# Edge rows added in pairs on VectorE before the one-hot products, in a graph-attention layer on one core

## The chip, the cores and the metric

The kernel runs on one core of one Trainium2 chip. The metric is the device time of one launch in microseconds; the time before is the median of three runs. Engines are named as the profile names them: PE is TensorE, DVE is VectorE, ACT is ScalarE, POOL is GpSimd, SP is SyncE.

## The reference

12,500 nodes with 128 features and 412,500 directed edges, sorted by their target node. A layer norm and a ReLU precede a graph attention with four heads of 32; the result is added to x.

```python
h = relu(layernorm(x)) @ W_node.T             # per head: 32 columns
att = sum(concat(h[src], h[dst], edge_attr @ W_edge.T) * a)   # one number per edge and head
att = where(att > 0, att, 0.2 * att)
m = maximum(segment_max(att, dst), 0)
ex = exp(att - m[dst])
denom = segment_sum(ex, dst) + (num_edges - deg) * exp(-m)
out = x + segment_sum(ex / denom[dst] * h[src], dst)
```

The sources are random, so h[src] is a gather of 412,500 rows.

## The kernel before

**Lead-in.** All 98 blocks of 128 nodes are loaded, measured with bn_stats on DVE, normalized on ACT and POOL, transposed on PE, passed through a ReLU on DVE, multiplied with the weights and written to a table in DRAM. A row of the table (ROW = 144 numbers) has, per head, 32 features, two ones and two parts of the attention. The lead-in is a software pipeline over units of three blocks, its order written out by hand: a unit is normalized and transposed three steps (`lag`) ahead of its product. Only when the table is complete can the first row be gathered.

**Batches.** The edges come in 461 chunks of 896. Seven chunks make a batch; there are 66 batches, the last with six chunks. Of a batch, POOL gathers the rows of the sources: one indirect DMA for each group of 128 edges, 49 in a batch (`gather`, L631), 3223 in all. Each reads its 128 row numbers from the tile `ends` in SBUF. Four buffers (`hs`) hold gathered batches, and POOL runs through batch after batch with one short memset (`gate`) between them, which waits for the products of the batch that had the buffer before.

When the rows of a batch have landed, DVE adds the attention parts (`logits`, L729), finds each node's highest attention with two scans (L739, L741), ACT takes the exponentials (L744), DVE makes a one-hot of each edge's target modulo 32 (`mark`, L699), weights the rows (`scatter`, L814), and PE multiplies the one-hot with the rows: seven groups, two products each, 14 in a batch (L819). The sums go to DRAM and come back turned (`pass_on`, `turn_sums`). `choose` picks the target's part of the next batch's attention by predicated copies (L606). DVE runs all of that in program order.

**Merge.** Two batches at a time, `merge` carries sums across chunks with a scan, writes each chunk's last value into two places (`put`, L919), and adds them with one DVE instruction per chunk at a column read from a register (L926). `finish` divides and adds x when a group of nodes is complete: L1002 multiplies with a factor in PSUM, L1005 adds two tiles in SBUF, L866 shifts the sums.

**Where tiles lie.** `exr`, `up` of the batches, `more`, `pa` and `z` are in PSUM; `hs`, `ends`, `acc`, `xg`, `a`, `hot` and `pick` are in SBUF. In the row `hs<-hs,exr` of L814 one input is therefore in SBUF and one in PSUM, in `xg<-xg,a` of L1005 both are in SBUF.

**The end.** The last batch is done in two parts (four groups of each chunk, then three), so that the first part's attention and sums run while the second part is still gathered.

Should a chunk break an assumption on the lists (sortedness, how far targets spread), a flag is raised and a slow loop over windows does the whole work again at the end.

Of the kernel before, what the change touches and what calls it, by code (L numbers as in the profile page):

```python
# [65 lines left out]
COUNTED = 24  # L66
FIRST = 2
# [58 lines left out]
def kernel(  # L126
# [3 lines left out]
    ends: bass.AP,  # L130
    dstc: bass.AP,
# [37 lines left out]
    lastm = const.tile([P, NC2, 2], U8, name="lastm")  # L169
# [28 lines left out]
    for b in range(NBT):  # L198
        if b == NBT - 1 or base_of(b + 1) > base_of(b):
            c = chunk_of(b + 1) - 1  # L200
            nc.gpsimd.memset(highest[:, c:c + 1], float(base_of(b) + WQ - 2))
# [35 lines left out]
    with (  # L237
# [50 lines left out]
        def extent(g):  # L288
# [7 lines left out]
            nc.sync.dma_start(pens[g * P:g * P + n, :], pen[:n, :])  # L296
            nc.vector.tensor_reduce(ext[:n, g, 0:1], dch[:n, :], AX.X, OP.min)
            nc.vector.tensor_reduce(ext[:n, g, 1:2], rise[:n, :], AX.X, OP.min)
            nc.vector.tensor_reduce(ext[:n, g, 2:3], dch[:n, :], AX.X, OP.max)
# [4 lines left out]
        sizes = [XS, XS, 2 * XS] + [XB] * ((NB - 4 * XS) // XB)  # L304
        sizes += [XS, NB - sum(sizes) - XS]
# [51 lines left out]
        def normalize(u):  # L357
            s = u.s
            u.hn = p2.tile([P, XS, D], F32, name="hn", bufs=4)
# [39 lines left out]
        def keep_near():  # L399

            pn = pp1.tile([P, H * P], F32, name="pn")[:NB, :].rearrange("p (h i) -> p h i", h=H)
# [18 lines left out]
        ahead, lag = 7, 3  # L420
# [3 lines left out]
        measure(units[1])  # L424
# [23 lines left out]
        def chunk_ranges():  # L448
# [4 lines left out]
            pb = [pp1.tile([P, H * P], F32, name="pn")[:, :NC2], pp1.tile([P, NC2], F32, name="pb")]  # L453
# [30 lines left out]
            yield  # L484
            nc.vector.tensor_tensor(qn, qn, later, op=OP.add)
# [6 lines left out]
            nc.vector.tensor_tensor(lastm[:, :, 1], last, later, op=OP.mult)  # L492
            nc.vector.tensor_tensor(lastm[:, :, 0], last, lastm[:, :, 1], op=OP.subtract)
# [3 lines left out]
        done = 2  # L497
        full = None
        for k in range(-lag, whole + 1):
# [3 lines left out]
            u = units[k + lag] if k + lag < whole else None  # L503
            if 0 <= k < whole:
                project(units[k])
            if u:
                normalize(u)
                turn(u)
                if u is u.s.units[-1]:
                    load_next()  # L510
            if full:
                write(full)
            full = keep_rows(units[k]) if 0 <= k < whole else None
            for _ in range(2):
                if done < min(k + ahead + 1, whole):
                    measure(units[done])
                    done += 1
            if u:
                keep_turned(u)
            for s in measured:  # L520
                root(s)
            measured.clear()
            if k == whole - 4:
                early += [index(b) for b in range(2, AHEAD)]
        keep_near()
        load_extents()
# [17 lines left out]
    here_ps = more_ps[:, LEVELS * T * CB:LEVELS * T * CB + MC * 2].rearrange("p (c j) -> p c j", j=2)  # L544
# [138 lines left out]
    def mark(s):  # L683

        if s.b < NBT - 1:
            s.hot = work.tile([P, T, CB, W], F32, name="hot", bufs=2)
        else:
            s.hot = work.tile([P, SB, CE], F32, name="eft").rearrange("p j e -> p (j e)")[
                :, :T * CB * W].rearrange("p (t q r) -> p t q r", q=CB, r=W)
        dk = work.tile([P, CB * T], I32, name="dk")  # L690
        dst = s.ends[:, :, 1, :]
        nc.vector.tensor_scalar(dk.rearrange("p (q t) -> p q t", t=T), dst, W - 1, None, op0=OP.bitwise_and)

        far = work.tile([P, CB * T], F32, name="far")
        nc.vector.tensor_scalar(far, away, float(W), float(W), op0=OP.is_ge, op1=OP.mult)
        key = work.tile([P, T * CB], F32, name="key")
        nc.vector.tensor_tensor(key.rearrange("p (t q) -> p q t", q=CB), far.rearrange("p (q t) -> p q t", t=T),
                                dk.rearrange("p (q t) -> p q t", t=T), op=OP.add)
        nc.vector.tensor_tensor(s.hot.rearrange("p t q r -> p (t q) r"), rows_ps[:, None, :].to_broadcast([P, T * CB, W]),  # L699
                                key[:, :, None].to_broadcast([P, T * CB, W]), op=OP.is_equal)  # L700

    def weigh(s):
# [7 lines left out]
        weigh_part(s, 0, EARLY if s.b == NBT - 1 else T)  # L710

    def open_weights(s):

        s.zst = work.tile([P, T, R], F32, name="zst")
        s.att = work.tile([P, BUF], F32, name="a")[:R, :CE]
        s.up = ps.tile([P, BANKS * 512], F32, name="up")[:R, :CE]
        s.m = work.tile([P, BUF], F32, name="m")[:R, :CE]
        s.both = work.tile([P, 2, T, R], F32, name="both")

    def weigh_part(s, t0, t1):  # L720

        zst, att, up, m, both = s.zst, s.att, s.up, s.m, s.both
        own = s.hs.rearrange("p (t q) (h k) -> p t q h k", t=T, h=H)[:, t0:t1, :s.chunks, :, AW - 1]
        e0, e1 = t0 * P, t1 * P

        def grouped(what, g):
            return what.rearrange("r (t g i) -> r g t i", g=NQT, i=R)[:, g, t0:t1, :]

        nc.vector.tensor_tensor(logits[:, t0:t1, :s.chunks * H].rearrange("p t (q h) -> p t q h", h=H),  # L729
                                own, s.pick[:, t0:t1, :s.chunks, :H], op=OP.add)  # L730
        nc.vector.transpose(zst[:, t0:t1, :].rearrange("p t i -> p (t i)"),
                            logits[:, t0:t1, :].rearrange("p t i -> p (t i)"))
# [9 lines left out]
        on_half(s, nc.vector.tensor_tensor(att[:, e0:e1], z, mp, op=OP.subtract))  # L742
        for g in range(NQT):
            nc.scalar.activation(both[g * R:(g + 1) * R, 0, t0:t1, :], grouped(att, g), AF.Exp)  # L744
        for g in range(NQT):
            nc.vector.scalar_tensor_tensor(both[g * R:(g + 1) * R, 1, t0:t1, :], grouped(s.pen[:, 1:], g), -1.0 / BIG,  # L746
                                           grouped(up, g), op0=OP.mult, op1=OP.mult)
        if t1 - t0 == T:
            nc.vector.transpose(both_ps.rearrange("p w t r -> p (w t r)"), both.rearrange("p w t r -> p (w t r)"))
        else:  # L750
            for w in range(2):
                nc.vector.transpose(both_ps[:, w, t0:t1, :].rearrange("p t r -> p (t r)"),
                                    both[:, w, t0:t1, :].rearrange("p t r -> p (t r)"))
        nc.vector.tensor_copy(own, both_ps[:, 1, t0:t1, :s.chunks * H].rearrange("p t (q h) -> p t q h", h=H))
# [17 lines left out]
    def first_part(s):  # L772
# [6 lines left out]
        weigh(s)  # L779
        s.first = sum_part(s, *spans[0])  # L780
# [27 lines left out]
    def scatter(s):  # L808
# [3 lines left out]
        for t0, t1 in ((0, FIRST), (FIRST, T)):  # L812
# [3 lines left out]
            for t in range(t0, t1):  # L816
                for g in range(2):
# [598 lines left out]
```

## Time and profile before

| | us |
|---|---|
| three runs | 4144.61, 4147.24, 4148.44 |
| median | 4147.24 |
| the profiled execution | 4155.16 |
| its span, first to last instruction | 4153.4 |
| DVE busy | 2397.3 (58%) |
| POOL busy | 3093.9 (74%) |
| PE busy | 1362.1 (33%) |
| ACT busy | 461.3 (11%) |

The profile's durations come from the one profiled execution, whose time is 7.9 us over the median of the runs and 1.8 us over its own span. "Idle before" in a row is the time in which the engine did nothing ahead of these instructions, with what ended it.

### The profile page before, as it was taken

To read this page: it belongs to the slowest core of one execution; us is meant where nothing else is said; L and a number is where in the kernel's file an instruction comes from. 1 tells how busy PE (TensorE), PEld (TensorE's weight loads), DVE (VectorE), ACT (ScalarE), POOL (GpSimd) and SP (SyncE) were. 2 spreads that over 40 slices of the span, in tenths; PEclk is the share of its full clock that TensorE was granted. 3 is DMA by queue.
4 is the path that set the end of the run, shared out by engine and by line. 5 is a ranking of instruction groups with operands and counts; after the bars stand their busy time and mean duration, and the time that the engine had idled before them with its cause. 6 is when DMAs were issued, how large, how long until landed. Compare 5 with 4: busy or idle time off the path is not lost.

```text
span 4153.4 us, 18432 instructions
## 1 busy us (share of the span) xinstructions
PE 1362.1 (33%) x3375; PEld 539.4 (13%) x3375; DVE 2397.3 (58%) x3550; ACT 461.3 (11%) x654; POOL 3093.9 (74%) x3393
## 2 busy tenths in 40 slices
PE   5332333233233233233323323323323322332331
PEld 4111111011011011111101101101101110110111
DVE  7456465456556457646555655654655654665576
ACT  4011011011101101101101110110110110111011
POOL 4777777777777777777777777777777777777775
PEclk8665666666666666566666666656656666666665
DMA  6443443443343444334444434444434434434442
GB/s 182 137 113 97 108 121 94 112 118 101 103 121 99 112 112 118 100 108 114 95 112 119 105 103 114 103 110 113 114 100 114 117 91 112 119 99 113 119 106 55
DMA packets 417256, 457.11 MB, mean 110 GB/s; under 512 B 240614, under 2 KB 324794, under 8 KB 417132
## 3 DMA queue, kind: packets, MB, share of 16 engines
q0 software_dynamic: 103136, 237.83, 24.2%
q1 hardware_dynamic: 199232, 165.73, 14.0%
q10 hardware_dynamic: 114764, 52.30, 4.7%
q14 instruction: 96, 0.79, 0.1%
q8 instruction: 28, 0.46, 0.0%
HBM read 406.51 MB, written 49.05 MB: 110 GB/s over the span
## 4 chain that ended last, share of the span: by engine, by line
POOL 73%; issue 24%; DVE 2%; PE 0%; DMA 0%; ACT 0%; POOLq 0%; ACTq 0%; SPq 0%; DVEq 0%
POOL hs L631 73%; DVE stats L331 0%; DVE hT L377 0%; POOL gate L627 0%; DMA turned<-wide 0%; DVE acc L926 0%; PE pt L372 0%; PE ph L382 0%; PE pa L803 0%; ACTq L841 0%; POOLq L631 0%; DMA hs<-table,ends 0%; DVE dif L340 0%; DVE tot L337 0%; DVE dif L341 0%
## 5 line engine op out<-in xcount | busy, mean ns | idle before, releaser
L631 POOL DMA_INDIRECT hs<-table,ends x3223 | 3059.0, 949 | 990.6 <-issue 975.6
L819 PE MATMUL pa<-hs,hot 128*128 128x504 f32 x1820 | 929.5, 676 | 2673.1 <-DVE hs L814 2673.1
L729 DVE TENSOR_TENSOR logits<-hs,pick 128x196 f32<-128x196 f32 x65 | 32.4, 499 | 1497.8 <-DVEq L648 1497.8
L819 PEld LDWEIGHTS pa<-hs,hot 128*128 128x128 f32 x1820 | 396.4, 222 | 3198.4 <-issue 3166.3
L814 DVE TENSOR_TENSOR hs<-hs,exr 128x1848 f32<-128x1848 f32 (+1 forms) x130 | 451.6, 3516 | 0.0
L744 ACT ACTIVATE both<-a 32x224 f32<-32x224 f32 (+2 forms) x268 | 103.2, 385 | 2593.7 <-DVE a L742 2583.4
L679 PE MATMUL z<-eft,wa 128*32 128x512 f32 (+1 forms) x792 | 319.6, 547 | 6.3 <-DMA eft<-in_ef 6.3
L606 DVE COPY_PREDICATED pick<-more,pick 128x1568 f32<-128x1568 int32 (+3 forms) x260 | 253.6, 975 | 8.9
L606 DVE COPY_PREDICATED pick<-more,lw 128x3136 f32<-128x3136 int32 x65 | 241.3, 3712 | 9.5 <-ACT pick L590 3.8
L590 ACT COPY pick<-lw 128x3136 f32<-128x3136 f32 x65 | 182.4, 2806 | 11.5 <-ACTq L648 9.9
L926 DVE TENSOR_TENSOR acc<-acc,up 128x70 f32 x461 | 105.2, 228 | 71.0 <-issue 52.0
L739 DVE TENSOR_TENSOR_SCAN up<-pen_sb,z 32x896 f32<-32x896 f32 (+1 forms) x67 | 133.6, 1994 | 2.3
L741 DVE TENSOR_TENSOR_SCAN m<-pen_sb,up 32x896 f32<-32x896 f32 (+1 forms) x67 | 132.6, 1979 | 2.3
L699 DVE TENSOR_TENSOR hot<-exr,key 128x1568 f32<-128x1568 f32 x65 | 116.5, 1792 | 2.3
L734 DVE TENSOR_TENSOR up<-z,zst 32x224 f32<-32x224 f32 (+2 forms) x268 | 104.3, 389 | 13.8
L679 PEld LDWEIGHTS z<-eft,wa 128*32 128x32 f32 x792 | 79.5, 110 | 242.1 <-issue 235.0
L746 DVE SCALAR_TENSOR_TENSOR both<-pen_sb,up 32x224 f32<-32x224 f32 (+2 forms) x268 | 100.2, 374 | 4.3
L856 ACT COPY r<-turned 128x245 f32<-128x245 f32 x65 | 41.5, 639 | 339.0 <-ACTq L648 295.9
L738 DVE TENSOR_TENSOR z<-up,a 32x896 f32<-32x896 f32 (+1 forms) x67 | 72.3, 1080 | 2.3
L742 DVE TENSOR_TENSOR a<-z,m 32x896 f32<-32x896 f32 (+1 forms) x67 | 71.7, 1070 | 2.3
L737 DVE TENSOR_SCALAR a<-up 32x896 f32<-32x896 f32 (+1 forms) x67 | 71.3, 1064 | 2.3
L676 PE MATMUL z<-eft,wa 128*64 128x512 f32 (+1 forms) x132 | 64.6, 571 | 21.3 <-DMA eft<-in_ef 21.3
(181 smaller groups left out, 900.3 us busy)
## 6 DMA issues: line engine op xcount, KB each, us to landing
eft<-in_ef SPq DMA_DIRECT2D x33, 1792.0 KB, 8.2
hs<-table,ends POOLq DMA_INDIRECT x3223
eft<-in_ef SPq DMA_DIRECT2D x33, 1344.0 KB
wide<-stage ACTq DMA_DIRECT2D x65, 504.0 KB, 2.9
lw<-near SPq DMA_DIRECT2D x461, 64.0 KB
pen_sb<-pens SPq DMA_DIRECT2D x66, 98.1 KB
table<-rows ACTq DMA_DIRECT2D x9, 648.0 KB, 3.6
xg<-in_x SPq DMA_DIRECT2D x52, 112.0 KB, 6.1
```

Of the source, the lines that this page charges most:

```text
L590: nc.scalar.copy(s.pick[:, :, :s.chunks, :], lw[:, None, :s.chunks, :n].to_broadcast([P, T, s.chunks, n]))
L606: nc.vector.copy_predicated(s.pick[:, :, :s.chunks, :n], bit[:, :, :, None].to_broadcast([P, T, s.chunks, n]), more)
L631: load = nc.gpsimd.indirect_dma_start(out=s.hs[:, t * CB + q, :], out_offset=None, in_=table[:, :], in_offset=bass.IndirectOffsetOnAxis(ap ...
L679: s.made = own_half(s, nc.tensor.matmul(s.z[:, part], wa3[:, j + s.b % 2 * (SB + 1), :], s.eft[:, j, part], start=False, stop=(j == NEXT - ...
L699: nc.vector.tensor_tensor(s.hot.rearrange("p t q r -> p (t q) r"), rows_ps[:, None, :].to_broadcast([P, T * CB, W]), key[:, :, None].to_br ...
L734: on_half(s, nc.vector.tensor_tensor(grouped(up, g), grouped(s.z, g), zst[g * R:(g + 1) * R, t0:t1, :], op=OP.add))
L739: on_half(s, nc.vector.tensor_tensor_scan(up[:, e0:e1], s.pen[:, e0:e1], z, 0.0, op0=OP.add, op1=OP.max))
L741: nc.vector.tensor_tensor_scan(mp[:, ::-1], s.pen[:, e1:e0:-1], up[:, e0:e1][:, ::-1], 0.0, op0=OP.add, op1=OP.max)
L744: nc.scalar.activation(both[g * R:(g + 1) * R, 0, t0:t1, :], grouped(att, g), AF.Exp)
L814: nc.vector.tensor_tensor(rows, rows, ex_ps[:, t0:t1, :CB * H, None].to_broadcast([P, t1 - t0, CB * H, HB]), op=OP.mult)
L819: scattered[s.b] = nc.tensor.matmul(wide_ps[:, g, :], s.hot[:, t, g * NEXT:g * NEXT + SB, :].rearrange("p q r -> p (q r)"), flat[:, at:at ...
L926: nc.vector.tensor_tensor(sums, sums, put[:, i0 + i, :, :], op=OP.add)
```

## The change

1. **Lists.** For all but the last batch, the host lays the edges of a chunk out so that a partition's seven edges are neighbours in the sorted order (edge 7p + t instead of 128t + p). The number of gathers is unchanged. The edges' attention on the other side of the transpose is reordered with strided views (`grouped`).
2. **Products.** As neighbours mostly share a target, and a partition's seven edges change target at most once (checked by a new flag in `extent`), DVE adds the rows of edges 1, 3, 5 onto those of 0, 2, 4; the products of edges 0, 2, 4 and 6 follow. Where the two of a pair differ, the odd rows, kept by a 0/1 factor (`split`), are added up, and a fifth product moves them from the first target to the last: its one-hot is the difference of those of edge 6 and edge 0. Five rounds of two products replace seven. `mark` makes four one-hots and a difference instead of seven one-hots.
3. **Weights.** The four DVE additions of attention per batch become four ACT copies and one DVE addition; the four exponentials on ACT become four ACT copies and one exponential after the transpose back; the four products with the penalty become one.
4. **Merge.** A table of zeros and ones (`rel`, `one`) over eight columns replaces the writes per chunk: per batch one product of 128x1960, one reduction to 128x280, one addition to `acc`.
5. **Order.** `mark` moves ahead of the scans, `choose` of the next batch ahead of the transpose back.
6. **Lead-in.** An older form: two steps ahead instead of three, fewer buffers, other sizes of the first and last groups, other order within a step.

```diff
-        sizes = [XS, XS, 2 * XS] + [XB] * ((NB - 4 * XS) // XB)
-        sizes += [XS, NB - sum(sizes) - XS]
+        sizes = [XS, 2 * XS] + [XB] * ((NB - 3 * XS) // XB)
+        sizes += [2 * XS, NB - sum(sizes) - 2 * XS]
...
-            u.hn = p2.tile([P, XS, D], F32, name="hn", bufs=4)
+            u.hn = p2.tile([P, XS, D], F32, name="hn", bufs=3)
...
-            pt = pps.tile([P, XS, P], F32, name="pt", bufs=3)
+            pt = pps.tile([P, XS, P], F32, name="pt")
...
-            u.hT = p2.tile([P, XS, P], F32, name="hT", bufs=5)
+            u.hT = p2.tile([P, XS, P], F32, name="hT", bufs=3)
...
-        ahead, lag = 7, 3
+        ahead = 8
...
     def mark(s):
...
+            nc.vector.tensor_tensor(s.hot[:, ROUNDS - 1, :, :], s.hot[:, ROUNDS - 2, :, :], s.hot[:, 0, :, :], op=OP.subtract)
+            s.split = work.tile([P, T // 2, CB], F32, name="split")
+            nc.vector.tensor_tensor(s.split, dk[:, 1::2, :], dk[:, 0:T - 1:2, :], op=OP.not_equal)
...
         for g in range(NQT):
-            on_half(s, nc.vector.tensor_tensor(grouped(up, g), grouped(s.z, g),
-                                               zst[g * R:(g + 1) * R, t0:t1, :], op=OP.add))
+            nc.scalar.copy(grouped(s, s.pair[:, 0:1, :], g, t0, t1)[:, 0], s.zst[g * R:(g + 1) * R, t0:t1, :])
...
+        on_half(s, nc.vector.tensor_tensor(up[:, e0:e1], z, att[:, e0:e1], op=OP.add))
...
+        nc.vector.scalar_tensor_tensor(mp, s.pen[:, e0 + 1:e1 + 1], -1.0 / BIG, up[:, e0:e1], op0=OP.mult, op1=OP.mult)
         for g in range(NQT):
-            nc.scalar.activation(both[g * R:(g + 1) * R, 0, t0:t1, :], grouped(att, g), AF.Exp)
-        for g in range(NQT):
-            nc.vector.scalar_tensor_tensor(both[g * R:(g + 1) * R, 1, t0:t1, :], grouped(s.pen[:, 1:], g), -1.0 / BIG,
-                                           grouped(up, g), op0=OP.mult, op1=OP.mult)
+            nc.scalar.copy(both[g * R:(g + 1) * R, :, t0:t1, :], grouped(s, s.pair, g, t0, t1))
...
+        nc.scalar.activation(ex_ps[:, t0:t1, :], ex_ps[:, t0:t1, :], AF.Exp)
...
     def scatter(s):
...
-            for t in range(t0, t1):
-                for g in range(2):
...
+        tiles = flat.rearrange("p (t c) -> p t c", t=T)
+        add_to(s, T - 1, ROUNDS - 2, True)
+        nc.vector.tensor_tensor(tiles[:, 0:T - 1:2, :], tiles[:, 0:T - 1:2, :], tiles[:, 1::2, :], op=OP.add)
+        for k in range(ROUNDS - 2):
+            add_to(s, 2 * k, k)
+        odd = s.hs.rearrange("p (t q) c -> p t q c", t=T)[:, 1::2, :, :]
+        nc.vector.tensor_tensor(odd, odd, s.split[:, :, :, None].to_broadcast([P, T // 2, CB, ROW]), op=OP.mult)
+        for k in range(1, T // 2):
+            nc.vector.tensor_tensor(tiles[:, 1, :], tiles[:, 1, :], tiles[:, 2 * k + 1, :], op=OP.add)
+        add_to(s, 1, ROUNDS - 1)
+
+    def add_to(s, t, k, start=False):
...
+        for g in range(2):
+            at = (t * CB + g * NEXT) * ROW + g * HALFROW
+            scattered[s.b] = nc.tensor.matmul(
+                wide_ps[:, g, :], s.hot[:, k, g * NEXT:g * NEXT + SB, :].rearrange("p q r -> p (q r)"),
+                flat[:, at:at + SPAN], start=start, stop=(k == ROUNDS - 1))
...
-            for i, v in enumerate(got):
-                sums = acc[:, ds(v, 2), :]
-                nc.vector.tensor_tensor(sums, sums, put[:, i0 + i, :, :], op=OP.add)
...
+        for i, v in enumerate(got):
+            spread_out = work.tile([P, 2, BUF], F32, name="a").rearrange("p w c -> p (w c)")[
+                :, :JW * AW * each].rearrange("p (j d c) -> p j d c", j=JW, d=AW)
+            ends_of = val[:, :, step + i * CB * step:1 + (i * CB + each) * step:step]
+            nc.vector.tensor_tensor(spread_out, ends_of[:, None, :, :].to_broadcast([P, JW, AW, each]),
+                                    one[:, i, :, None, :each].to_broadcast([P, JW, AW, each]), op=OP.mult)
+            nc.vector.tensor_reduce(put, spread_out, AX.X, OP.add)
+            sums = acc[:, ds(v, JW), :]
+            nc.vector.tensor_tensor(sums, sums, put, op=OP.add)
```

More of the change, by code (lines that the diff above doesn't have):

```diff
@@ L502 @@
             rooted.clear()
-            u = units[k + lag] if k + lag < whole else None
             if 0 <= k < whole:
                 project(units[k])
[L506 to L519, printed above, removed]
+            if k + 2 < len(units):
+                normalize(units[k + 2])
             for s in measured:
@@ L695, in mark @@
[L695 to L698, printed above, removed]
+            s.hot = work.tile([P, ROUNDS, CB, W], F32, name="hot", bufs=2)
+            dk = work.tile([P, T, CB], I32, name="dk")
+            nc.vector.tensor_scalar(dk.rearrange("p t q -> p q t"), s.ends[:, :, 1, :], W - 1, None, op0=OP.bitwise_and)
@@ L1033, in close @@
             return
[L1034 removed]
+        merge(first, chunk_of(first), chunks_of(first, last), *merged.pop(first))
         for b0, n, behind in parts():
```

197 lines of the change are left out of this document (122 added, 75 removed).

## The prediction

> **What bounds the kernel now.** I read the page first: the span, the chain of work that ended last, and the costliest groups.
>
> ```profile
> span 4153.4 us, 18432 instructions
> ...
> POOL 73%; issue 24%; DVE 2%; PE 0%; DMA 0%; ACT 0%; POOLq 0%; ACTq 0%; SPq 0%; DVEq 0%
> ...
> L631 POOL DMA_INDIRECT hs<-table,ends x3223 | 3059.0, 949 | 990.6 <-issue 975.6
> L729 DVE TENSOR_TENSOR logits<-hs,pick 128x196 f32<-128x196 f32 x65 | 32.4, 499 | 1497.8 <-DVEq L648 1497.8
> ```
>
> POOL's gathers and the issue gaps between them are 97% of the chain. DVE, the engine on which most of the change lies, stands idle 1497.8 us ahead of its first instruction of a batch, 23 us in each of 65, because the rows have not landed. The line of the gathers says how rigid this is:
>
> ```profile
> L631 POOL DMA_INDIRECT hs<-table,ends x3223: 943/947/1841, 77.4 to 4118.1; - x190
> ```
>
> 3222 steps from 77.4 to 4118.1 are 1.254 us each; the median gather is 0.947 and the gap 975.6/3222 = 0.303, together 1.250. So the time is lead-in 77.4, then 3223 gathers back to back, then a tail of 4153.4 - 4119.1 = 34 us. Four products fewer on PE, or less DVE work, buy nothing in the middle. The question is whether anything in the change touches the gathers, and a few of them did take up to 1841 ns. The timeline shows when.
>
> ```profile
> 1231.99 1.09 DVE L1002 TENSOR_TENSOR a<-acc,exr 128x896 f32<-128x896 f32 x1
> 1232.59 0.95 POOL L631 DMA_INDIRECT hs<-table,ends  x1 [0.30 <-issue]
> 1233.11 1.09 DVE L1005 TENSOR_TENSOR xg<-xg,a 128x896 f32<-128x896 f32 x1
> 1233.84 1.18 POOL L631 DMA_INDIRECT hs<-table,ends  x1 [0.30 <-issue]
> ```
>
> The gather that starts inside L1002 (one input in SBUF, `exr` in PSUM) takes 0.95; the one that starts inside L1005 (both inputs in SBUF) takes 1.18. It ends at 1235.02, 0.82 after L1005's end at 1234.20. A second place, with a copy right behind:
>
> ```profile
> 863.82 1.09 DVE L1005 TENSOR_TENSOR xg<-xg,a 128x896 f32<-128x896 f32 x1
> 863.92 1.82 POOL L631 DMA_INDIRECT hs<-table,ends  x1 [0.31 <-issue]
> 864.83 0.56 DVE L866 COPY acc<-acc 128x770 f32<-128x770 f32 x1
> ```
>
> ```profile
> 619.53 0.55 DVE L866 COPY acc<-acc 128x770 f32<-128x770 f32 x1
> 619.73 1.16 POOL L631 DMA_INDIRECT hs<-table,ends  x1 [0.30 <-issue]
> ```
>
> The gather of 863.92 ends at 865.74, again 0.83 after L1005's end (864.91), although L866 had begun by then, and L866 does hold a gather that starts inside it (1.16 at 619.73, end 0.81 after the copy's). So: a gather that starts inside such an instruction is held until that instruction ends, gets through before the next one, and ends 0.82 later, as if it had started 0.12 before the end. L1005 itself loses nothing. The long weighting products, with `exr` in PSUM, hold nothing:
>
> ```profile
> 4086.25 6.94 DVE L814 TENSOR_TENSOR hs<-hs,exr 128x1848 f32<-128x1848 f32 x2
> 4086.83 0.95 POOL L631 DMA_INDIRECT hs<-table,ends  x1 [0.30 <-issue]
> 4088.08 0.95 POOL L631 DMA_INDIRECT hs<-table,ends  x1 [0.30 <-issue]
> ```
>
> Thus POOL loses, for a DVE instruction of length L with two SBUF inputs, L - 0.12 - s, where s is the time from its start to the next gather's start; nothing if that is negative. For a random phase s is between 0 and 1.25, 0.63 in the mean.
>
> **The change part by part.** Its new instructions with two SBUF inputs need lengths.
>
> ```profile
> L926 DVE TENSOR_TENSOR acc<-acc,up 128x70 f32 x461 | 105.2, 228 | 71.0 <-issue 52.0 <-DVE acc L926 4.7
> ...
> L919 DVE TENSOR_TENSOR up<-up,more 128x476 f32<-128x476 f32 x62 | 59.9, 967 | 2.1
> ...
> L1005 DVE TENSOR_TENSOR xg<-xg,a 128x896 f32<-128x896 f32 x13 | 14.2, 1095 | 0.5
> ...
> L1005 DVE TENSOR_TENSOR xg<-xg,a 128x512 f32<-128x512 f32 x1 | 0.7, 691 | 0.0
> ```
>
> L1005's two sizes give (1095 - 691)/384 = 1.05 ns an element and 0.15 us besides: 3.33 us for 3024 elements, 2.21 for 1960, 1.21 for 1008, 0.39 for 224.
>
> *The pairs (the term that decides).* Each of 65 batches gets four in a row on `hs`, all from SBUF: the pair addition (3024), the product with `split` (3024), and two additions of 1008. The first costs POOL 3.33 - 0.12 - 0.63 = 2.58 (1.96 to 3.21 by the phase, which is likely the same in every batch, since DVE starts each at the landing of its last gather). The held gather ends 0.83 after it, the next starts 0.30 later, at 1.13; the second instruction begins some 0.03 after the first (L1002 to L1005), so s is 1.10 and the loss 3.33 - 0.12 - 1.10 = 2.11. At the third, s is 1.10 again against 1.21 - 0.12 = 1.09: free by a hair, as is the fourth (0 to 0.1 each if that is off). Sum 4.69 a batch, 65 x 4.69 = **305 us**, all on POOL's chain, since nothing can catch up a gather.
>
> [...]
>
> *The merge.* The product of 1960 per batch reads `val` and `one`, both SBUF: 2.21 - 0.12 - 0.63 = 1.46 (0.84 to 2.09). The views step through short runs, and L919, with a strided view, took 967/476 = 2.0 ns an element; at that rate it is 4.1 us and 3.3 lost. I take the lower, as the innermost run of seven is contiguous. 64 of the 66 fall while POOL still gathers: 64 x 1.46 = **93 us** (54 to 211). The reduction reads one input, `acc` is added to PSUM: no loss; the additions of L926, with one PSUM input too, go at no gain on the chain.
>
> *Small ones.* The one-hot difference (0.39 us) holds a gather only when one starts in its first 0.27: 0.27²/2.5 = 0.03 a batch. With the third and fourth additions above and three passes of 468 in the lead-in: **3 us**.
>
> *DVE itself.* How much room it has:
>
> ```profile
> 620.00:1110.00 490.00, 163.79 (x336) 61.55 (x336) 276.36 (x374) 50.31 (x65) 371.69 (x400) 0.65 0.42 109
> ```
>
> Eight batches of 61.3 us hold 34.6 us of DVE each. Added: 9.1 for the four, and per batch 2.2 + 2.2 + 0.4 in the merge in place of 7 x 0.228 + 0.97; the shorter one-hots and single additions return one or two. Some 46 of a period that becomes 67: hidden. If this cover were gone, DVE would set the period, and it is 20 us away. `choose` and `mark` ahead of the transpose delay the rest of the batch's DVE work but no gather: the buffer POOL needs next belongs to a batch three back. ACT's eight copies lie beside that. The products removed on PE wait for DVE anyway: nothing.
>
> *Lead-in.*
>
> ```profile
> 20.00:30.00 10.00, 7.28 (x53) 6.35 (x54) 8.25 (x42) 6.87 (x17) 3.93 (x9) 1.00 0.58 163
> ```
>
> DVE is busy 8.25 of 10 here and keeps the same instructions, so a better order could give at most 0.18 x 60 = 10 us; an order with two steps instead of three between transpose and product, and fewer buffers, can only wait more: I take +4, with -5 and +20 as ends. The new passes of `extent` run while POOL gathers.
>
> *Tail.* After the last batch's first rows land, DVE and ACT take turns:
>
> ```profile
> 4102.10 0.33 DVE L729 TENSOR_TENSOR logits<-hs 128x96 f32<-128x96 f32 x1 [8.63 <-DVEq L648]
> ...
> 4108.75 1.15 DVE L746 SCALAR_TENSOR_TENSOR both<-pen_sb,up 32x128 f32<-32x128 f32 x4
> 4108.75 0.31 ACT L744 ACTIVATE both<-a 32x128 f32<-32x128 f32 x1 [5.30 <-DVE a L742]
> ...
> 4115.64 0.64 ACT L856 COPY r<-turned 128x245 f32<-128x245 f32 x1 [5.62 <-ACTq L648]
> ...
> 4119.92 1.20 DVE L919 TENSOR_TENSOR up<-up,more 128x238 f32<-128x238 f32 x2
> 4121.15 1.81 DVE L926 TENSOR_TENSOR acc<-acc,up 128x70 f32 x7
> ```
>
> The 9.1 us of additions of the batch before fit the 8.63 of idle time, the more so as the rows land later. Then ACT's four copies (some 0.31 each) come ahead of one addition (about 0.7 for 512), in place of four additions: +1; the penalty product now comes ahead of ACT's copies and a transpose ahead of the exponential, and the transfers of `turn_sums` are behind that on ACT: +3 until L856. The merge: 2.2 + 2.2 + 0.4 for 1.2 + 1.8: +1.7. The second part pays about 2 and its merge 1.5. Sum **+9** (2 to 14).
>
> **Sum.** Against the profiled execution: 4155.2 + 305 + 93 + 3 + 4 + 9 = 4569. That execution is 7.9 over the median of the runs, so the median should come to 4147.2 + 414 = **4561**. About 0.2%, 8 us, is what a measurement of this kernel can tell from no change.
>
> **The rivals.**
>
> *Each of the four costs its whole length.* POOL is not let in between neighbouring instructions, or a waiting DVE instruction takes the next turn. Then the four cost 9.1 - 0.12 - 0.63 = 8.3 a batch: 4147 + 540 + 93 + 16 = **4796**. Against it: the gather of 863.92 got through before L866, and L1005 took the same 1.09 wherever gathers lay. For it: no row shows two such instructions of equal kind in a row.
> [...] Chance 0.10.
>
> *No loss: the other side.* The place is the four instructions on `hs` and the product in the merge, the price of each zero, if a gather's reading of `ends` can be served beside them; it decides as soon as gathers started inside them still take 0.95. What L1005 showed would then be something of L1005 alone, such as the stores issued after it. Then the time is 4147 + 13 - 7 = **4153** with little of lead-in and tail, not slower.
> [...] Chance 0.04.
>
> *It does not do what it says.* If the lists broke the new flags, the slow loop would do everything again, thousands of us. In the reference's lists, which I counted, no partition changes target twice and no batch spans more than eight windows. Chance 0.01.
>
> **How the numbers follow.** The forecast has 0.85. Its own ends: 65 x (1.96 + 2.0) + 64 x 0.84 - 5 + 2 gives 4455; 65 x (3.21 + 2.3) + 211 + 20 + 14 gives 4750. The corner needs the strided rate and the worst phase together, so I cut it: 4455 to 4700 holds about 0.8 of all cases, with the two main rivals outside. Faster 0.01, within 0.2% 0.03 (the second rival, which could come out a little on either side), slower 0.96.
>
> **What would show it.** In the profile after, the gathers keep a median of 0.947 but their mean rises from 0.949 to about 1.07 (0.949 + 401/3223), with two long ones a batch, ending 0.82 after the pair addition and the `split` product, and one in each merge; the step between gathers is 1.38 instead of 1.25; DVE's idle time ahead of the attention parts stays near 20 us a batch; POOL and issue still make nearly the whole chain. I am wrong on the mechanism if gathers inside those instructions take 0.95, on its size if none passes between them or if the merge's product takes over 3 us.

## The result, and the profile after

The changed kernel takes 4515.01 us (median of four runs, 4512.01 to 4517.71) against 4146.65 for the kernel before beside it: a ratio of 1.0888 (1.0869 to 1.0907), 368 us slower. The forecast was 4561 in a range of 4455 to 4700.

The page after, its lines of the span, of the gathers and of DVE's wait ahead of a batch, then the line of the gathers (shortest, median and longest of one in ns, first and last start):

```profile
span 4514.5 us, 16833 instructions
...
L657 POOL DMA_INDIRECT hs<-table,ends x3223 | 3408.2, 1057 | 984.8 <-issue 984.8
L757 DVE TENSOR_TENSOR logits<-hs,pick 128x196 f32<-128x196 f32 x65 | 32.4, 499 | 1249.0 <-DVEq L674 1249.0
```

```profile
L657 POOL DMA_INDIRECT hs<-table,ends x3223: 940/944/4081, 75.0 to 4464.4; - x190
```

The median gather is 0.944 us, as before (0.947); the mean has gone from 0.949 to 1.057. POOL still waits for nothing but its own issue gaps. DVE still idles 1249/65 = 19 us a batch. So the loss is inside single gathers, and the timeline of a batch shows in which:

```profile
1035.61 3.37 DVE L861 TENSOR_TENSOR hs<-hs 128x3024 f32<-128x3024 f32 x1
1035.65 0.95 POOL L657 DMA_INDIRECT hs<-table,ends  x1 [0.31 <-issue]
...
1036.90 2.91 POOL L657 DMA_INDIRECT hs<-table,ends  x1 [0.30 <-issue]
...
1039.02 3.31 DVE L865 TENSOR_TENSOR hs<-hs,split 128x3024 f32<-128x3024 f32 x1
...
1040.11 3.04 POOL L657 DMA_INDIRECT hs<-table,ends  x1 [0.30 <-issue]
...
1042.36 2.45 DVE L867 TENSOR_TENSOR hs<-hs 128x1008 f32<-128x1008 f32 x2
...
1043.45 0.94 POOL L657 DMA_INDIRECT hs<-table,ends  x1 [0.30 <-issue]
```

```profile
1048.79 2.19 DVE L981 TENSOR_TENSOR a<-up,one 128x1960 f32<-128x1960 f32 x1
1049.79 2.01 POOL L657 DMA_INDIRECT hs<-table,ends  x1 [0.30 <-issue]
1051.01 2.20 DVE L983 TENSOR_REDUCE up<-a 128x280 f32<-128x1960 f32 x1
1052.10 0.94 POOL L657 DMA_INDIRECT hs<-table,ends  x1 [0.30 <-issue]
```

Three long gathers a batch. The first ends at 1039.81, 0.83 after the pair addition's end (1038.98); the second at 1043.15, 0.82 after that of the `split` product; the third at 1051.80, 0.82 after that of the merge's product. Between two neighbours a gather gets through, although they are 0.04 us apart. The gather begun in the reduction L983 (one input) takes 0.94.

"Held time" below is the time of each of the 3223 gathers over 0.945 us, put down to the DVE instruction that ended 0.82 us before the gather. In the changed kernel it is 366.0 us, in the kernel before 9.8. The rows bear the sum out: (1057 - 944) ns x 3223 = 364. By line: pair addition 143.0, `split` product 135.9, merge's product 69.0, bits of `choose` (L623) 9.0, the rest 9.

How the spans differ, from the starts and ends of the first and last gather:

| us | before | after | difference |
|---|---|---|---|
| to the first gather | 77.4 | 75.0 | -2.4 |
| first gather to the last one's end | 4041.7 | 4390.3 | +348.6 |
| behind the last gather | 34.3 | 49.2 | +14.9 |
| span | 4153.4 | 4514.5 | +361.1 |

Of the 348.6, +356.2 are held time and -0.6 gaps between gathers; the gathers that were not held are shorter than in the profiled run of before (943.8 ns against 946.1 in the mean), which makes -7.0. The run of before was also 8.5 over its median and that of after 1.2 over its own: 361.1 + 7.3 = 368.

### The profile page after: what moved, and what is told of

It is laid out like the page before. It is cut to its first block, busy times and chain, and to the rows that moved or that the text cites. A ratio compares the mean times of both kernels' runs of the same rounds, so it can differ in the third digit from the quotient of the medians.

```text
span 4514.5 us, 16833 instructions
## 1 busy us (share of the span) xinstructions
PE 1153.9 (26%) x2855; PEld 427.3 (9%) x2855; DVE 3024.8 (67%) x3045; ACT 805.7 (18%) x988; POOL 3443.0 (76%) x3394
## 5 line engine op out<-in xcount | busy, mean ns | idle before, releaser
L657 POOL DMA_INDIRECT hs<-table,ends x3223 | 3408.2, 1057 | 984.8 <-issue 984.8
L875 PE MATMUL pa<-hs,hot 128*128 128x504 f32 x1300 | 720.4, 715 | 3229.3 <-DVE hs L857 3222.6
L875 PEld LDWEIGHTS pa<-hs,hot 128*128 128x128 f32 x1300 | 284.8, 232 | 3657.0 <-issue 3509.6
L762 ACT COPY a<-zst 32x224 f32<-32x224 f32 (+2 forms) x268 | 155.6, 581 | 1754.5 <-DVE zst L759 1707.7
L779 ACT COPY both<-a 32x448 f32<-32x448 f32 (+2 forms) x268 | 263.1, 982 | 471.5 <-DVE a L777 459.3
L861 DVE TENSOR_TENSOR hs<-hs 128x3024 f32<-128x3024 f32 x65 | 217.8, 3351 | 2.2
L865 DVE TENSOR_TENSOR hs<-hs,split 128x3024 f32<-128x3024 f32 x65 | 215.0, 3308 | 2.2
L867 DVE TENSOR_TENSOR hs<-hs 128x1008 f32<-128x1008 f32 x130 | 157.0, 1208 | 4.5
L983 DVE TENSOR_REDUCE up<-a 128x280 f32<-128x1960 f32 x66 | 145.1, 2198 | 2.2
L981 DVE TENSOR_TENSOR a<-up,one 128x1960 f32<-128x1960 f32 x66 | 144.4, 2188 | 0.0
L775 DVE TENSOR_TENSOR_SCAN a<-pen_sb,up 32x896 f32<-32x896 f32 (+1 forms) x67 | 132.6, 1979 | 2.3
```

Of the source, the lines that this page charges most:

```text
L657: load = nc.gpsimd.indirect_dma_start(out=s.hs[:, t * CB + q, :], out_offset=None, in_=table[:, :], in_offset=bass.IndirectOffsetOnAxis(ap ...
L762: nc.scalar.copy(grouped(s, s.pair[:, 0:1, :], g, t0, t1)[:, 0], s.zst[g * R:(g + 1) * R, t0:t1, :])
L779: nc.scalar.copy(both[g * R:(g + 1) * R, :, t0:t1, :], grouped(s, s.pair, g, t0, t1))
L861: nc.vector.tensor_tensor(tiles[:, 0:T - 1:2, :], tiles[:, 0:T - 1:2, :], tiles[:, 1::2, :], op=OP.add)
L865: nc.vector.tensor_tensor(odd, odd, s.split[:, :, :, None].to_broadcast([P, T // 2, CB, ROW]), op=OP.mult)
L867: nc.vector.tensor_tensor(tiles[:, 1, :], tiles[:, 1, :], tiles[:, 2 * k + 1, :], op=OP.add)
```

## Experiments

Theory: a gather that starts inside a DVE instruction with two inputs in SBUF waits for the end of that one instruction, so the loss is length - 0.12 - s, with s from the instruction's start to the gather's. Rivals: the loss comes from something else in the new code (its order, its waits, more DVE work); or all time in which DVE reads two inputs from SBUF is lost, however it is cut.

Seven of the twelve runs were on two chips on which the kernel before takes 4762 and 4770 us ("late chips" below); the other five were on chips where it takes 4145 and 4147 ("usual chips"). On a late chip POOL waits for buffers (462.1 us at the gate below), which hides what single gathers lose: 306.9 us held show as 21 us of time (experiment 1). Of those runs only held time, and where the first gather starts, is read. Three rows of one kernel, first on a late chip (`g6_before_older_leadin`), then two of them on a usual one (`h6_before_older_leadin`), where the gate has no idle time (0.0):

```profile
L637 POOL MEMSET gate<- 128x1 f32 x62 | 6.5, 105 | 462.1 <-remote 462.1
L739 DVE TENSOR_TENSOR logits<-hs,pick 128x196 f32<-128x196 f32 x65 | 30.9, 475 | 100.2 <-DMA hs<-table,ends 93.3 <-issue 2.5 <-DVEq L658 1.2
L744 DVE TENSOR_TENSOR up<-z,zst 32x224 f32<-32x224 f32 (+2 forms) x268 | 104.3, 389 | 745.3 <-remote 497.3 <-issue 227.5 <-DVE zst L741 8.2
```

```profile
L739 DVE TENSOR_TENSOR logits<-hs,pick 128x196 f32<-128x196 f32 x65 | 32.4, 498 | 1485.7 <-DVEq L658 1485.7
L744 DVE TENSOR_TENSOR up<-z,zst 32x224 f32<-32x224 f32 (+2 forms) x268 | 104.2, 389 | 14.5 <-DVE zst L741 0.9
```

The expectations of the later runs put the late chips down to rows that land late. These rows say otherwise: there DVE waits only 100.2 us for gathered rows, not 1485.7, and stands idle in the middle of a batch instead (745.3 us ahead of L744, not 14.5). So it is DVE that comes late to rows that lie ready, and buffers come free late. What delays it there is open.

**1. Kernel before, with its weights in SBUF.** The attention weights that `scatter` multiplies with move from PSUM to SBUF; nothing else changes.

```diff
-    both_ps = bank[:, :2 * T * R].rearrange("p (w t r) -> p w t r", w=2, t=T)
+    both_ps = work.tile([P, 2, T, R], F32, name="both_sb")
```

> The kernel before, unchanged but for one tile: the turned weights (448 numbers a partition), which lay in PSUM, lie in SBUF. The two weighting products of a batch (1848 and 4620 elements, 2.07 and 4.96 us, L814) then read both inputs from SBUF; no instruction is added. Theory (two SBUF inputs): first product 2.07 - 0.12 - 0.63 = 1.32 (0.70 to 1.95 by the phase), second 4.96 - 0.12 - 1.10 = 3.74, together 5.06 a batch, times 65 = 329: 4147 + 329 = 4476 (4436 to 4517). Rival (the price belongs to the pair additions, to their traffic or to DVE's load): 4147, since neither changes.

> The kernel before with the turned weights in SBUF instead of PSUM, again, on a chip on which issuing the gathers sets the time (the kernel before at about 4147). The first run of it had 306.9 us of holding at L814, as forecast (329), on a chip where the rows landed so late that holding was hidden. Theory (two SBUF inputs hold gathers, and held time is on the path where issue sets the pace): 4147 + 307 to 329 = 4454 to 4476. Rival (holding is hidden here too, the changed kernel lost its time by something else, such as DVE's load): 4147. If the kernel before takes about 4760 again, the chip is of the other kind, and only the held time in the trace can be read.

On a late chip 4783.56, with 306.9 us held at L814; on a usual one 4470.04 against 4147.19 (1.078, 1.0748 to 1.0811), as expected. Its line of the gathers, and a batch of its timeline:

```profile
L631 POOL DMA_INDIRECT hs<-table,ends x3223 | 3375.0, 1047 | 988.7 <-issue 975.0 <-DMA near<-turned 13.8
...
L814 DVE TENSOR_TENSOR hs<-hs,both_sb 128x1848 f32<-128x1848 f32 (+1 forms) x130 | 452.2, 3521 | 0.0
```

```profile
1021.16 6.96 DVE L814 TENSOR_TENSOR hs<-hs,both_sb 128x1848 f32<-128x1848 f32 x2
1021.75 2.30 POOL L631 DMA_INDIRECT hs<-table,ends  x1 [0.30 <-issue]
1024.36 4.58 POOL L631 DMA_INDIRECT hs<-table,ends  x1 [0.31 <-issue]
```

L814 takes the same time as before (3521 ns against 3516), DVE's work is unchanged (busy 2394.0 us against 2397.3), and 321.8 us are held at it: 323 us lost by where one small operand lies. This has none of the new code, so order and waits of the new code are not needed for such a loss.

**2. Changed kernel, `split` and `one` in PSUM.** The two factors get room in the bank of `more`.

```diff
-            s.split = work.tile([P, T // 2, CB], F32, name="split")
+            s.split = split_ps
...
-        one = work.tile([P, MB, JW, CB], F32, name="one")
+        one = one_ps
```

> The changed kernel with two small tiles moved from SBUF to PSUM: the 0/1 factor of the pairs (21 numbers a partition) and the 0/1 table of the merge (112). The product with split (L865) and the merge's product (L981) then have one input in SBUF; lengths, order and results stay. Theory (a DVE instruction with two SBUF inputs holds the gather that starts inside it until its end): the trace of the changed kernel has 135.9 us of holding at L865 and 69.0 at L981, and both go; the third instruction (1008 elements), which was free because a gather had just been let through, now meets one with s about 0.27: 1.21 - 0.12 - 0.27 = 0.82, times 65 = 53. Time 4515 - 136 - 69 + 53 = 4363. Rival 1 (any long DVE work on the rows that are being gathered slows POOL, by the traffic to SBUF): nothing changes on hs, 4515, or 4446 if only the merge's share goes. Rival 2 (DVE's longer batch sets the period): 4515.

> The changed kernel with the pairs' factor and the merge's table in PSUM, again, on a chip on which issuing the gathers sets the time. Theory: of the changed kernel's held 356 us over the kernel before, 136 (L865) and 69 (merge) go, some 42 to 53 come at the two additions of 1008, and the pair addition keeps 143: 4515 - 205 + 42 to 53 = 4352 to 4363. Rival (traffic or load): 4515.

4797.42 on a late chip; 4382.77 on a usual one (1.0569, 1.0538 to 1.06). The batch:

```profile
1009.90 3.38 DVE L865 TENSOR_TENSOR hs<-hs 128x3024 f32<-128x3024 f32 x1
1009.93 0.94 POOL L661 DMA_INDIRECT hs<-table,ends  x1 [0.30 <-issue]
1011.18 2.91 POOL L661 DMA_INDIRECT hs<-table,ends  x1 [0.30 <-issue]
1013.31 3.30 DVE L869 TENSOR_TENSOR hs<-hs,more 128x3024 f32<-128x3024 f32 x1
1014.40 0.94 POOL L661 DMA_INDIRECT hs<-table,ends  x1 [0.31 <-issue]
1015.64 0.94 POOL L661 DMA_INDIRECT hs<-table,ends  x1 [0.30 <-issue]
1016.65 2.45 DVE L871 TENSOR_TENSOR hs<-hs 128x1008 f32<-128x1008 f32 x2
1016.89 1.78 POOL L661 DMA_INDIRECT hs<-table,ends  x1 [0.30 <-issue]
```

Held at the `split` product and the merge's product: nothing, in both runs. But the additions of 1008, free in the changed kernel, now hold 54.2 us: no gather is held right ahead of them, so the next one starts at another phase (s is 0.24; 1.21 - 0.12 - 0.24 = 0.85, and the row shows 1.78 - 0.94 = 0.84). Another 9.8 us are held at the addition of `finish`, which held none in the changed kernel, and the tail is 57.3 us instead of 49.2; I had counted neither, hence 20 to 30 us over the expectation.

**3. All four with one SBUF input each.** On top of 2, the pair addition and the additions of 1008 become reductions into a tile of their own; three gather buffers instead of four make room.

```diff
-RING = 4
+RING = 3
...
-        nc.vector.tensor_tensor(tiles[:, 0:T - 1:2, :], tiles[:, 0:T - 1:2, :], tiles[:, 1::2, :], op=OP.add)
+        pairs = work.tile([P, T // 2 + 1, CB * ROW], F32, name="pairs")
+        nc.vector.tensor_reduce(pairs[:, :T // 2, :], tiles[:, :T - 1, :].rearrange("p (u v) c -> p u c v", v=2), AX.X, OP.add)
...
+        nc.vector.tensor_reduce(pairs[:, T // 2, :], tiles[:, 1::2, :].rearrange("p u c -> p c u"), AX.X, OP.add)
```

> As the kernel with both factors in PSUM, and the pair addition and the two additions of 1008 become reductions that read one view of the rows (6048 elements in pairs, 3024 in threes) and write a tile of their own; three row buffers instead of four make room for it. DVE does more work than in the changed kernel: 6048 elements at 1.05 to 2.0 ns are 6.5 to 12 us for the first, 3.3 to 6 for the last, in place of 3.3 and 2.4. Theory (two SBUF inputs): no held gathers on hs or in the merge, so 4147 - 2 (lead-in, first gather at 75.0 instead of 77.4) + 15 to 20 (tail) + 10 (the small ones, L623 and the like) = 4170 to 4175, faster than the changed kernel by 340 although DVE works longer. Rivals 1 and 2 (traffic of the rows, length of DVE's batch): 4515 or more.

> The kernel with every new instruction reading at most one input from SBUF, again, on a chip on which issuing the gathers sets the time. Its first run had 17 us of holding in all, none at the pairs or the merge, with DVE busy 3309 us against 3025 in the changed kernel. Theory: 4147 - 2 (lead-in) + 15 to 20 (tail) + 7 (holding over the 10 us that the kernel before has) = 4167 to 4172. Rival (DVE's load or the traffic of the rows sets the changed kernel's time): 4515 or more.

4748.60 on a late chip, a ratio of 0.9939 (0.9909 to 0.9969) to the kernel before there; 4204.74 on a usual one (1.014, 1.011 to 1.0169), which is 33 us over the upper end of the expectation.

```profile
L661 POOL DMA_INDIRECT hs<-table,ends x3223 | 3066.5, 951 | 985.3 <-issue 984.7
...
L866 DVE TENSOR_REDUCE pairs<-hs 128x3024 f32<-128x6048 f32 x65 | 424.4, 6529 | 7.2 <-DVE hs L861 0.9
```

```profile
1031.52 6.53 DVE L866 TENSOR_REDUCE pairs<-hs 128x3024 f32<-128x6048 f32 x1
1032.74 0.95 POOL L661 DMA_INDIRECT hs<-table,ends  x1 [0.30 <-issue]
1033.99 0.94 POOL L661 DMA_INDIRECT hs<-table,ends  x1 [0.30 <-issue]
```

The reduction is twice as long as the addition and holds nothing, in both runs; the mean gather is back at 951, and the gathers' stretch at 4048.4, 7 us over the kernel before. This is the clearest run: more DVE work, in the same place and order, and the loss is gone. The gathers begun inside the reduction above take 0.95 and 0.94 us. What I missed is the end: DVE waits for rows only 654.8/65 = 10 us a batch now, and at the end it has fallen behind. The last whole batch's weighting begins at 4124.05, during the last gather (4123.9 to 4124.8); in the changed kernel it begins at 4435.88, 28 us ahead of the last gather. The tail is 79.8 us instead of 49.2.

**4. Twelve pieces.** Pair addition and `split` product each as twelve instructions of 252 elements.

```diff
+        for i in range(0, T - 1, 2):
+            for c in range(0, CB * ROW, CB * ROW // 4):
+                part = slice(c, c + CB * ROW // 4)
+                nc.vector.tensor_tensor(tiles[:, i, part], tiles[:, i, part], tiles[:, i + 1, part], op=OP.add)
...
```

> The changed kernel with the pair addition and the product with split each cut into twelve instructions of 252 elements (about 0.42 us each), both inputs still in SBUF; all else the same. Theory (a held gather passes at the end of each instruction): a gather is held for at most 0.42 - 0.12 = 0.3, 0.13 in the mean; six to eight gathers fall into the 8 to 11 us of pieces, so 0.8 to 1.0 a batch in place of 4.3, and up to 0.8 more for the two additions of 1008 behind them, whose phase moves: 4515 - 65 x 2.9 = 4330, or 4290 without the latter, though DVE needs 2 to 4 us more a batch. Rival (POOL loses the whole time during which DVE reads two inputs, whoever waits): the time rises with DVE's, to 4600 and above.

> The changed kernel, with the pair addition and the product with split each cut into twelve instructions of 252 elements instead of one of 3024; the same arithmetic. Theory (a gather is held only until the instruction in which it starts ends, and passes before the next): a piece of some 0.4 us can hold a gather only if it starts in its first 0.28 us, so the 143 + 136 us of the two fall to some 15 + 25. The phase behind them changes, so the two additions of 1008, free in the changed kernel by a hair, may cost up to 0.75 us a batch, 49 us. The merge's 69 stays. 4515 - 279 + 40 + 49 = about 4325, at most 4340. Rival A (the gathers lose the whole time in which DVE reads two inputs from SBUF, however it is cut): the sum of the twelve is longer than the one, 4600 or more. Rival B (the loss is in the order or the waits around these instructions, not in their length): 4515.

> The changed kernel with the pair addition and the product with split cut into twelve instructions of 252 elements each, on a chip where the rows of the kernel before land in time. Theory (a gather is held only by the instruction in which it starts, and only to that one's end): of the 143 + 136 us at the two some 17 + 24 stay, the additions of 1008 come to some 49, the merge to some 77: 4515 - 279 + 41 + 49 + 8 = about 4334, 4320 to 4350. Rival (the time in which DVE reads two inputs from SBUF is lost however it is cut): 4600 or more.

4883.08 and 4871.28 on late chips, with 15.4 + 24.4 and 16.8 + 23.9 held at the pieces; 4332.51 on a usual one (1.0451, 1.0431 to 1.047), with 4334 expected.

```profile
1062.02 4.06 DVE L864 TENSOR_TENSOR hs<-hs 128x252 f32<-128x252 f32 x12
1062.18 1.07 POOL L657 DMA_INDIRECT hs<-table,ends  x1 [0.30 <-issue]
1063.55 1.02 POOL L657 DMA_INDIRECT hs<-table,ends  x1 [0.30 <-issue]
...
1069.96 2.45 DVE L873 TENSOR_TENSOR hs<-hs 128x1008 f32<-128x1008 f32 x2
1070.18 1.81 POOL L657 DMA_INDIRECT hs<-table,ends  x1 [0.30 <-issue]
```

The same additions take 4.06 us instead of 3.37, and lose 0.08 to 0.13 per gather instead of 2.2 in one: held 18.4 + 14.5 for the two instead of 143.0 + 135.9. The additions of 1008 cost 50.9, since the phase at them has changed. This rules out that the whole time with two SBUF inputs is lost: what counts here is how long a single instruction runs (4.06/12 = 0.34 us against 3.37).

**5. A filler of one us ahead of the pair addition.** DVE sets an unused tile to zero while it has 19 us idle a batch.

```diff
+        nc.vector.memset(work.tile([P, 1120], F32, name="filler"), 0.0)
```

> The changed kernel with one instruction more: DVE sets an unused tile of 128x1120 to zero (about 1.0 us, no input from SBUF) right ahead of the pair addition. Theory (the loss depends on the phase between DVE and the gathers, and the pair addition's is locked because DVE starts a batch at the landing of its rows): in the changed kernel the next gather starts 0.04 us after the pair addition and mostly slips through, so the loss is 2.20 on average; 1.0 us later it starts some 0.29 us after it in every batch and loses 3.31 - 0.12 - 0.29 = 2.9. That is 0.7 x 65 = 45 us more, about 4560, although DVE is idle for 19 us in each batch. Rival (idle time of DVE hides what is added to it, the loss is no matter of phase): 4515. A loss of 2.0 or less there (4500 or below) would say that the phase does not hold as read.

This ran only on a late chip (4741.69), so its held time alone is read: 240.4 at the pair addition instead of 143.0. That is 97 us more, not the expected 45.

```profile
1009.61 5.06 POOL L657 DMA_INDIRECT hs<-table,ends  x1 [0.30 <-issue]
...
1009.70 0.99 DVE L861 MEMSET filler<- 128x1120 f32 x1 [0.18 <-issue]
1010.61 3.25 DVE L862 TENSOR_TENSOR hs<-hs 128x3024 f32<-128x3024 f32 x1
```

A gather that starts 0.09 ahead of the memset is held through the memset and the whole pair addition: it ends at 1014.67, 0.81 after the latter (1013.86). So the filler did not only move the phase: gathers are held from the memset on, and none gets through before the pair addition. A memset by itself does not do that. In the kernel before, the gather begun 0.38 us into the memset of `acc` takes 0.94; in `f2_all_one_input` the addition L761, both inputs in SBUF, follows that memset at once, and the gather begun at the same point takes 1.56 and ends 0.78 after L761 (12 of 13 times; the 13th time another instruction follows, and the gather takes 0.95):

```profile
1234.95 0.88 DVE L867 MEMSET acc<- 128x980 f32 x1 [0.27 <-DVE acc L866]
1235.33 0.94 POOL L631 DMA_INDIRECT hs<-table,ends  x1 [0.30 <-issue]
```

```profile
1246.81 0.88 DVE L929 MEMSET acc<- 128x980 f32 x1 [0.27 <-DMA hs<-table,ends]
1247.19 1.56 POOL L661 DMA_INDIRECT hs<-table,ends  x1 [0.30 <-issue]
1247.60 0.37 DVE L761 TENSOR_TENSOR logits<-hs,pick 128x196 f32<-128x196 f32 x1
```

So an instruction with two SBUF inputs right behind a memset holds gathers from before its own start; how it does so is not shown. The idle time did not hide the filler, as expected; the size of 45 missed, and the run doesn't test the phase alone.

**6. The kernel before with the older lead-in and no hold in `finish`.** This is the kernel before with the changed kernel's lead-in, and with the product that `finish` adds in L1005 kept in PSUM.

```diff
-        wgt = pool.tile([P, BUF], F32, name="a")[:, :GB * 4 * HD].rearrange("p (q d) -> p q d", d=HD)
+        wgt = pool.tile([P, BUF], F32, name="a") if wide is None else wide.tile([P, BANKS * 512], F32, name="up")
+        wgt = wgt[:, :GB * 4 * HD].rearrange("p (q d) -> p q d", d=HD)
...
-        ahead, lag = 7, 3
+        ahead = 8
```

> The kernel before with two things: the changed kernel's lead-in, and the product with the weights in finish put into PSUM, so that the addition of L1005 reads one input from SBUF and one from PSUM. Theory: the first gather starts at 75.0 instead of 77.4 (-2.4), the held gathers at L1005 go (-3.4): 4147 - 5.8 = about 4141, ratio 0.9986. Rival (the start of the first gather in the changed kernel came from its other parts or from chance, and the wait moves elsewhere): 4144 to 4151, a ratio of 0.999 to 1.001.

> The kernel before with the changed kernel's lead-in, and with the product with the weights in finish put into PSUM, so that the addition of L1005 reads one input from SBUF and one from PSUM; on a chip where the rows land in time. Theory: first gather at 74.7 instead of 77.4, no gather held at L1005 (3.4 us): 4147 - 6 = 4141, ratio 0.9986. Rival (what is gained ahead is waited for elsewhere): a ratio of 0.9995 to 1.0005.

On a late chip 4767.93, a ratio of 0.9993 (0.9974 to 1.0011): not to be told apart. On a usual one 4141.55 against 4145.28, 0.9990 (0.9981 to 0.9999): 3.7 us faster, as far as the interval tells (0.4 to 8). That interval takes in the 0.9986 of the theory and most of the rival's 0.9995 to 1.0005, so it does not decide between them.

```profile
L641 POOL DMA_INDIRECT hs<-table,ends x3223: 940/944/1846, 76.5 to 4105.7; - x190
```

No gather is held at the addition of `finish` any more (3.4 us in the kernel before), and the first starts at 76.5 instead of 77.4: 4.3 together, by one profile each.

## Why the prediction was right, and where it was off

**Right.** The mechanism, and the place: gathers hold the chain (3408.2 us of them and 984.8 of issue gaps in a span of 4514.5), a gather begun in an instruction with two SBUF inputs is held to its end (2.91 us in the pair addition, 3.04 in the `split` product, 2.01 in the merge's product), and passes before the next. The mean gather was to rise to about 1.07 (1.057), the step to 1.38 (4389.4/3222 = 1.362), the idle time before a batch to stay near 20 us (19). The `split` product was put at 2.11 a batch and took 135.9/65 = 2.09: there the phase was derived (the held gather before it sets s), and the derivation held. The additions of 1008, "free by a hair", were free (the 130 gathers begun in them take 0.94 to 0.96 us); experiments 2 and 4 show that the hair mattered, 51 to 54 us once the instruction ahead holds nothing. DVE's cover held, and the missing PE products brought nothing: PE idles 3222.6 us ahead of L875 until DVE has weighted the rows. The rule itself was put too narrowly: the prediction's own row of L866, a copy with one input, holds a gather (1.16 us), and in the changed kernel that copy (L924) holds one all 13 times, 4.3 us in all. One small slip changes nothing: 276.36/8 is 34.5, not 34.6.

**The rivals.** That each of the four costs its whole length: the gather at 1036.90 passed before the `split` product, and experiment 4 has gathers pass at every piece. That nothing is lost: 3.04 and 2.91 us. The slow loop did not run.

**Mis-sized: the pair addition, 2.20 instead of 2.58, and the merge, 1.08 instead of 1.46.** Both used the mean phase of 0.63, and the text itself said that the phase is likely the same in every batch. It is nearly so. At the pair addition a gather starts within 0.06 us of it in 53 of 65 batches: in 44 of these it slips through and the one after it loses about 1.96, in 9 it is held and loses 3.1. In 8 more the gather ahead starts some 0.3 us before it, and the next loses 2.2; the other 4 lose 2.5 to 2.9. So the low end of "1.96 to 3.21" is the usual one. At the merge's product s is 1.0, as in the timeline above: 2.19 - 0.12 - 1.0 = 1.07. Together 305 + 93 became 279 + 69, 50 us less. The strided rate that stretched the range did not come: 2.19 us, as taken.

**Missed: 9.0 us at L623.** Its row in the kernel before (L597) held nothing; with `choose` moved, a gather starts in it in most batches. The sum had only the new instructions, not those whose phase moves.

**Lead-in: -2.4 instead of +4.** Here the sign was wrong. In ten other profiles with the older lead-in the first gather starts at 74.6 to 76.6, in the three with the newer one (the kernel before, and twice experiment 1) at 76.6 to 77.4, so the gain is between 0 and 3 us. Why two steps and fewer buffers are not worse was not tried.

**Tail: +14.9 instead of +9.** The step that failed is "the 9.1 us of additions of the batch before fit the 8.63 of idle time":

```profile
4399.32 0.17 DVE L949 TENSOR_SCALAR mc<-r 128x7 f32<-128x7 f32 x1 [10.24 <-ACT r L912]
...
4449.53 2.45 DVE L867 TENSOR_TENSOR hs<-hs 128x1008 f32<-128x1008 f32 x2
...
4452.31 0.33 DVE L757 TENSOR_TENSOR logits<-hs 128x96 f32<-128x96 f32 x1
...
4457.05 0.69 DVE L770 TENSOR_TENSOR up<-z,a 32x512 f32<-32x512 f32 x1 [4.06 <-ACT a L762]
```

DVE comes to the last batch's first part with no idle time: it had waited 10.24 us for the sums of an earlier batch and has run without a long break since then. The attention of that part starts 12.0 us before the last gather's start instead of 16.0: +4.0. From there to the copy of the weights it is 13.9 us instead of 8.7 (4466.20 - 4452.31 against 4110.77 - 4102.10), +5.2, as ACT's four copies (L762) start at 4455.76, behind the copy of `stage` (1.00 us from 4454.35); about 4 was forecast. The rest, with the longer merges, is +5.7, where 5.2 was forecast.

In sum: 414 were forecast, 368 measured. Pair addition and merge make -50 of the difference, L623 and the other short ones +5 (8 instead of 3), the lead-in -6, the tail +6. What the table shows beside that, gathers 2 ns shorter and the gaps, is undone to within 1 us by the two profiled runs' distances from their medians. That lead-in and tail cancel is luck; the two large terms carry the forecast, and both were too high.

## What to carry to other kernels

Where POOL's gathers set the pace, look at how the instructions on VectorE read. Here long ones with two inputs in SBUF held the next gather to their end (2.91 and 3.04 us instead of 0.94), though VectorE was idle a third of the time (busy 67% of the span). Three things took the hold away: one of the operands in PSUM (a small factor was enough: nothing held at the `split` product in experiment 2), a reduction with one input (0.94 to 0.95 inside it, experiment 3), and, for most of it, pieces well under the step from gather to gather (0.34 us against 1.25; 33 us held instead of 279, experiment 4). One input alone was no safe sign, as the copy L866 held gathers too (1.16 us): look at the trace. And count DVE's own time at the end of the kernel, where no idle time is left (a tail of 79.8 us in experiment 3 instead of 49.2). A phase that is set by the landing of rows was nearly locked (within 0.06 us in 53 of 65 batches): derive it, or take both ends, and expect that it moves for every instruction behind a change (the additions of 1008, free in the changed kernel, held 54.2 and 50.9 us in experiments 2 and 4).

## What the runs showed of the hardware that was not expected

- A DVE memset to SBUF held no gather by itself (those of `acc` in the kernel before, 13 gathers of 0.94 to 0.95 us), but with a pair addition right behind it gathers are held from the memset on (5.06 us for one gather).
- A copy from SBUF to SBUF (L866, one input, 0.56 us) holds gathers: 1.16 us for one that starts inside it, and 1.26 to 1.28 all 13 times in the changed kernel (L924).
- A gather that begins 0.01 to 0.04 us after the pair addition can pass: it takes 0.94 to 0.95, and the addition 3.35 to 3.38 instead of 3.31. DVE waits at most some 0.08 us, never for a whole gather.
- The gathers' own median was 0.947 in three profiles (the kernel before, `g3_twelve_pieces`, `g5_filler_ahead`) and 0.944 in the other eleven. In the first that makes some 7 us, near the 8.5 by which this profiled run lay above its median; that the one explains the other is not shown.
- The same kernel before takes 4145 to 4147 on some chips and 4762 to 4770 on others, where DVE comes late to a batch. There 306.9 us held in the gathers (experiment 1) show as 21 us.
- ACT's copies from 32 partitions of 448 numbers take 1.00 us each (median). Ahead of the transpose back of a whole batch (L784) DVE waits for them only once, 4.14 us in the last one; in the batches before, it has the next batch's `choose` to do meanwhile.
